# Layer 0 of a four-layer convolution network: the sums for dt over 32 columns of TensorE's array instead of 128

## The chip, the core and the metric

The kernel runs on one core of one Trainium2 chip. The time is device microseconds (us) of one execution, as the median of several; lower is better. Every time below comes from the timed runs or from one profiled execution; times inside that execution count from the start of its span.

## What is computed

The input x has 1024 channels of 64 x 64 pixels. Four layers follow each other, each of the form x = x + layer(groupnorm(x)). Only layer 0 is touched by the change. Cut to what matters, it is:

```
x_norm = layernorm2d(groupnorm(x))                       # per channel, over its 64 x 64 pixels
dt     = softplus(einsum('bsdc,c->bsd', x_norm, dt_w) + dt_b)   # one number for each channel s and image row d
log_a  = dt * (-exp(log_A))                              # one constant for each image row
out[t, r, c] = sum over j <= t of exp(cums[t, r] - cums[j, r]) * x_norm[j, r, c]   # cums = cumsum of log_a over channels
```

The channels are the sequence. out is a linear recurrence along them, h[t] = a[t, r] * h[t-1] + x_norm[t, r, :], with one decay a = exp(log_a) for each channel and image row, shared by the 64 pixels of the row. Layers 1 and 3 are 1024 x 1024 matrix products, layer 2 is a gated state-space layer with three such products; they take over at about 197 us and keep TensorE busy until the end.

## The kernel before, in words

**Tiles.** The image is split into two halves of 32 rows (TR = 32), and the channels into four groups of 256 (CH = 2 tiles of 128). One half of one channel group is a unit; there are NU = 8 units, and unit u is group u // 2, half u % 2. A unit's 2048 pixels form T0 = 16 pixel tiles of 128 pixels: 32 image rows times TW = 4 pixels of each. Four pixel tiles are a piece, so that there are NPIECE = 4 pieces to a unit and NI = 32 pieces in all. A piece is indexed i, with u = i // 4 and g = i % 4.

**Steps of a piece**, in the order in which they depend on each other:

- normalize (L590 on GpSimd, L592 on ScalarE) writes group-normed values xn for two pieces at a time, in two instructions of 128x1024.
- turn_in (L607, L613, L615): eight TensorE transposes of 128x128 turn xn so that pixels lie on partitions and channels along the free dimension. Four evictions of 128x256 apply the layer norm's weight and give XT, four pixel tiles of 256 channels. After the first pieces ScalarE does all four (L615).
- row_dt (L623): for each pixel tile one f32 product with a 128x128 matrix dtm as weights, accumulated over the 16 tiles of the unit into the left half of a PSUM bank called pd. dtm[t] holds dt_w on a block pattern (the constant "row": 1 where two pixels belong to the same image row), so that every one of a row's four partitions gets the row's sum. In the profile each such f32 product is two records, each with its weight load.
- decay, once a unit. Step 0: four ScalarE instructions on 128x256 (L632 to L635) make the two parts of softplus, e and m. Step 1: two TensorE products with the identity add them into the right half of the bank (L638). Step 2: ScalarE takes exp (L642, the first column alone, called first, and L643, the rest, into a PSUM tile called spread).
- begin, once a unit from the third on (L648, L651, GpSimd): multiplies the carried state by first and adds it to the first column of the unit's XT.
- scan (L658, VectorE): two 128x512 scans a piece, the recurrence itself, in place in XT.
- turn_back (L684; L676 and L682 in the last seven pieces): eight transposes back into PSUM (pb).
- add_up (L697, VectorE, two a piece; L695 on ScalarE for one of the two in the last pieces): adds the result to the image and sums it for the next layer's norm.
- squares (L709, ScalarE): one pass of 128x2048 for each channel tile of a finished unit, for the next layer's variance. Two a unit.

Beside this GpSimd sums weight blocks for layers 1 and 2 (L456 to L459, four instructions of 128x512 at a time), and VectorE takes the statistics (L567) for the norms of the later groups.

**Order.** The layer's scope sets the order by hand for TensorE, VectorE, ScalarE, GpSimd and the DMA queue of SyncE: each engine runs its instructions in the order in which the program issues them. The loop over i (from "for i in range(NI)") issues, for piece i: normalize for pieces i + 9 and i + 10 if i is odd; if g is 2, step 1 of the next unit's decay; scan(i); add_up(i - 1); turn_in(i + 7); row_dt(i + 6); turn_back(i); if g is 1, step 0 of the next unit's decay; if g is 2, step 2 of it and begin; one share of the weight sums; and, for g of 0 and 1 from the second unit on, squares of the unit before. The first seven pieces are turned in ahead of the loop, with their row_dt and the first unit's decay between them.

So pieces are turned in seven ahead of the scan, row_dt runs six ahead, and a unit's decay is ready two pieces before its first scan.

Of the kernel before, what the change touches and what calls it, by code (L numbers as in the profile page):

```python
# [10 lines left out]
F32 = mybir.dt.float32  # L11
# [9 lines left out]
P = 128  # L21
# [16 lines left out]
NK = -(-N // LT)  # L38
# [27 lines left out]
T0 = HN // P  # L66
TR = HW // 2
TW = HW // T0
CH = 2
NPIECE = T0 // 4  # L70
# [4 lines left out]
        ("Alog", S), ("D", 1), ("mob", 4 * HEADS), ("dbcb", HEADS * NF)]  # L75

_CST = [("ident", P), ("fold", LC), ("same", P), ("upto", LC), ("far", LC), ("eye", LC), ("eye8", S),
        ("from", 1), ("to", NK), ("group", P), ("row", P),
        ("gx", NT), ("gy", NT), ("flip", 7)]


def _columns(spec):
    at, out = 0, {}
    for name, n in spec:
        out[name] = slice(at, at + n)
        at += n
    return out, at
# [3 lines left out]
CST, NCST = _columns(_CST)  # L91
# [3 lines left out]
def tile_net(ctx: ExitStack, tc: tile.TileContext, x, par_d, cst_d, w_d, w2_d, dbcw_d, out):  # L95
    nc = tc.nc
# [414 lines left out]
    with tc.issue_after(exp_ln.ins), tc.tile_pool(name="l0x", bufs=2) as lx, \  # L511
# [4 lines left out]
        NU, NI = CT // CH * 2, CT // CH * 2 * NPIECE  # L516
# [27 lines left out]
        negA0 = const.tile([P, 2], F32, name="negA0")  # L544
        nc.scalar.activation(negA0, par[:, PAR["logA"]], AF.Exp)
        negA = const.tile([P, S], F32, name="negA")
        nc.scalar.activation(negA, par[:, PAR["Alog"]], AF.Exp)
        dtm = l0.tile([P, T0, P], F32, name="dtm", bufs=1)
        for t in range(T0):
            nc.gpsimd.tensor_scalar(dtm[:, t, :], cst[:, CST["row"]], pcol("dtw", t), None, ALU.mult)  # L550
        carry = l0.tile([P, 2, T0], F32, name="carry", bufs=1)
# [11 lines left out]
        def unit_stats(u, some):  # L563
            c, h = divmod(u, 2)
            for j in some:
                k, i = divmod(j, 4)
                nc.vector.bn_stats(stats[:, c * CH + k, 4 * h + i, :], half(u)[:, k, i * FB : (i + 1) * FB])  # L567
# [8 lines left out]
            nc.vector.tensor_copy(mean0[:, at], mean)  # L576
            nc.vector.tensor_scalar_mul(nmean0[:, at], mean, -1.0)

        xn, XT, PD, dt, PB = {}, {}, {}, {}, {}

        def normalize(n):

            u, j = divmod(n, 4)
            q, k = divmod(j, CH)
            scale, bias = norms[u // 2]
            xn[n] = l0.tile([P, 2, TR, HW // 4], F32, tag=f"xn{k}", name=f"xn{n}")
            part = half(u)[:, k, :].rearrange("p (r a g w) -> p a g r w", r=TR, a=2, g=2)[:, q]
            scale, bias = scale[:, k : k + 1], bias[:, k : k + 1]
            if n > LEAD + 4:
                nc.gpsimd.tensor_scalar(xn[n], part, scale, bias, ALU.mult, ALU.add)  # L590
            else:
                nc.scalar.activation(xn[n], part, AF.Identity, bias=bias, scale=scale)  # L592
# [24 lines left out]
        def row_dt(i):  # L617
            u, g = divmod(i, NPIECE)
            if g == 0:
                PD[u] = ps0.tile([P, FB], F32, tag="pd", name=f"pd{u}")  # L620
            for j in range(4):
                t = 4 * g + j
                nc.tensor.matmul(PD[u][:, : CH * P], dtm[:, t, :], XT[i][:, j, :], start=(t == 0), stop=(t == T0 - 1))  # L623

        def decay(u, step):

            if step == 0:
                e = l0.tile([P, CH * P], F32, tag="e", name=f"e{u}", bufs=1)
                m = l0.tile([P, CH * P], F32, tag="m", name=f"m{u}", bufs=1)
                dt[u] = e, m  # L630
                v = PD[u][:, : CH * P]
                nc.scalar.activation(e, v, AF.Abs, bias=pcol("dtb", 0))  # L632
                nc.scalar.activation(e, e, AF.Exp, scale=-1.0)
                nc.scalar.activation(m, v, AF.Relu, bias=pcol("dtb", 0))
                nc.scalar.activation(e, e, AF.Ln, bias=1.0)  # L635
            elif step == 1:
                for i, v in enumerate(dt[u]):
                    nc.tensor.matmul(PD[u][:, CH * P :], ident, v, start=(i == 0), stop=(i == 1))  # L638
            else:
                v, scale = PD[u][:, CH * P :], negA0[:, u % 2 : u % 2 + 1]  # L640
                if u > 1:
                    nc.scalar.activation(first_[u % 2], v[:, :1], AF.Exp, scale=scale)  # L642
                nc.scalar.activation(spread[u % 2][:, :, 1:], v[:, 1:].unsqueeze(1).to_broadcast([P, 2, CH * P - 1]),  # L643
                                     AF.Exp, scale=scale)
# [8 lines left out]
        def scan(i):  # L653
            u, g = divmod(i, NPIECE)
            c, h = divmod(u, 2)
            for j in (0, 2):
                xt = XT[i][:, j : j + 2, :].rearrange("p t c -> p (t c)")
                nc.vector.tensor_tensor_scan(xt, spread[h].rearrange("p t c -> p (t c)"), xt, 0.0, ALU.mult, ALU.add)  # L658
# [66 lines left out]
        turn_in(0, range(4))  # L725
        turn_in(1, range(4), "pb")
        row_dt(0)
        turn_in(2, (2, 3))
        row_dt(1)
        turn_in(3, (2, 3), "pb")  # L730
        row_dt(2)
        unit_stats(3, range(4))
        row_dt(3)
        decay(0, 0)
        normalize(4)
        unit_stats(3, range(4, 8))
# [16 lines left out]
        for i in range(NI):  # L753
            u, g = divmod(i, NPIECE)
            if i > 1 and i % 2 and i + LEAD + 2 < 4 * NU:
                normalize(i + LEAD + 2)
                normalize(i + LEAD + 3)
            if u + 1 < NU and g == 2:
                decay(u + 1, 1)
            scan(i)  # L760
            hand_on(i)
            if i == 0:
                finish_of(chain)
                chain = iter(())
            if i > 0:
                add_up(i - 1)
            if i == 0:
                for v, n in later.pop(0):
                    unit_stats(v, (n,))
                turn_in(5, (2, 3))  # L770
                turn_back(0)
                turn_in(6, (2, 3))
                row_dt(5)
            elif i + LEAD < NI:
                if i == 1:
                    row_dt(LEAD - 1)
                    turn_in(LEAD, (2, 3))
                    normalize(LEAD + 3)
                    normalize(LEAD + 4)
                turn_in(i + LEAD, ())  # L780
            if 0 < i <= NI - LEAD:
                row_dt(i + LEAD - 1)
            if i > 0:
                turn_back(i)
            if i == 0:
                normalize(LEAD + 1)
                normalize(LEAD + 2)
            if u + 1 < NU and g == 1:
                decay(u + 1, 0)
            if u + 1 < NU and g == 2:  # L790
                decay(u + 1, 2)
                if u > 0:
                    begin(u + 1)
            for v, n in later.get(i, ()):
                unit_stats(v, (n,))
            if i in (3, 11):
                chain = norm_chunk(2 if i == 3 else 3)
            next(chain, None)
            if i >= NPIECE and g < CH:
                squares(u - 1, g)  # L800
            if u == NU - 1 and 0 < g:
                for k in range(CH):
                    squares(u, k, g - 1)
            if g == 0 and u % 2 == 1:
                last_keep = keep(u // 2)
            if i == NPIECE + 1:
                bring(6)
            next(sums, None)
# [232 lines left out]
    with tc.manual_schedule(engines={E_.DVE, E_.PE, E_.Pool, E_.Activation}):  # L1041
        for i, _ in enumerate(pointwise("l1", W1, "b1", [3, 2] + EARLY, x0_d, x1_d, scores)):
# [35 lines left out]
    part, silus = {}, []  # L1078
# [21 lines left out]
    with tc.tile_pool(name="l2a", bufs=2) as pa, tc.tile_pool(name="l2a2", bufs=1) as pa2, \  # L1100
# [5 lines left out]
        row = pa2.tile([P, TPB, HEADS, NF2], F32, name="row", bufs=1)  # L1106
# [179 lines left out]
        with tc.manual_schedule(engines={E_.DVE, E_.PE, E_.Pool, E_.Activation}):  # L1286
# [3 lines left out]
            ends, i, chain, quiet = iter(()), -1, None, False  # L1290
# [71 lines left out]
    with tc.tile_pool(name="l2g", bufs=8) as pgat, tc.tile_pool(name="l2b", bufs=2) as pb, tc.tile_pool(name="l2r2", bufs=4) as prg, tc.tile_pool(name="l2h", bufs=1) as ph, \  # L1362
# [9 lines left out]
        rows, decay_, steps_ = {}, {}, {}  # L1372
# [463 lines left out]
def _constants():  # L1836
    c = np.zeros((P, NCST), np.float32)
    p, j = np.arange(P)[:, None], np.arange(P)[None, :]
    c[:, CST["ident"]] = p == j
    h, r = np.divmod(p, LC)  # L1840
    t = np.arange(LC)[None, :]
    c[:, CST["fold"]] = r == t
    c[:, CST["same"]] = h == j // LC
    c[:, CST["upto"]] = (t < S) | (r <= t)
    c[:, CST["far"]] = np.where((r >= S) & (t >= S) & (t < r), FAR, 0)
    c[:, CST["eye"]] = (r == t) & (r >= S)
    c[:KW, CST["eye8"]] = np.tile(np.eye(S), (KW // S, 1))
    c[:, CST["from"]] = HEADS * N + np.where(r < S, h * S + r, HEADS * S)
    c[:, CST["to"]] = HEADS * N + np.arange(NK)[None, :] * P + p
    c[:, CST["group"]] = (p // 32 == j // 32) / 32  # L1850
    c[:, CST["row"]] = p // TW == j // TW
    s = 1 - 2 * ((np.arange(P)[:, None] >> np.arange(6)[None, :]) & 1)
    s[:, 5] = 1
    c[:, CST["flip"]] = np.concatenate([s[:, :1], -s[:, :1], s[:, :5] * s[:, 1:]], axis=1)
    lin = _side()
    c[:, CST["gx"]] = np.tile(lin, HW).reshape(NT, P).T
    c[:, CST["gy"]] = np.repeat(lin, HW).reshape(NT, P).T
    return c
# [63 lines left out]
```

## Time and profile before

| what | value |
|---|---|
| median of 3 runs | 2637.35 us (2635.98 to 2638.56) |
| the profiled execution | 2640.7 us |
| its span | 2638.5 us, so 2.2 us lie around it |
| layer 0's last add_up ends | 189.8 us |
| first product of layer 1 starts | 197.0 us |
| busy share of the span: TensorE, VectorE, ScalarE, GpSimd | 97%, 69%, 40%, 46% |
| row_dt's products (L623) | 256 records, 64.1 us busy, all in the first 172 us |
| step 0 of decay (L632), starts for units 0 to 7 | 36.95, 58.61, 80.08, 97.75, 121.05, 138.72, 156.05, 171.28 us |

How to read the views used: the chain of waits goes back from the last instruction, at each step to what released it; its lines give start, length and what ran. The timeline lists an engine's instructions by start and length, with the idle time ahead of each and what ended it in square brackets. A table of windows gives the busy time of each engine in a stretch, with the number of records that began in it, the granted TensorE clock (PEclk, 1.00 is full) and the DMA share. A matmul's record lasts longer than its slot, since matmuls are pipelined: eight records of row_dt start one after the other over 1.73 us, while each is shown as about 0.4 us long. PE is TensorE, PEld its weight loads, DVE VectorE, ACT ScalarE, POOL GpSimd, SP SyncE.

### The profile page before, as it was taken

The page shows a single profiled execution, that of the slowest core. Times are in us where ns is not written, and L with a number is a line of the kernel's source. Part 1 is how long each engine was busy: PE and PEld are TensorE (multiplying, and loading weights), DVE is VectorE, ACT ScalarE, POOL GpSimd, SP SyncE. Part 2 cuts the span into 40 slices and gives each one's busy share as a digit, 9 for nine tenths or more (in the row PEclk, how much of TensorE's full clock was granted, in tenths as well). Part 3 has the DMA queues.
Part 4 walks back from the last instruction along what each step waited for, and adds up shares of the span by engine and source line. Part 5 has one row for each costly group of instructions (what it writes and reads, how often), then busy time and mean ns, then how long its engine had stood idle before and what let it go on. Part 6 is the DMA issues. An engine that isn't in the chain of part 4 may idle for free.

```text
span 2638.5 us, 30736 instructions
## 1 busy us (share of the span) xinstructions
PE 2560.3 (97%) x9588; PEld 1714.0 (65%) x9588; DVE 1819.1 (69%) x3776; ACT 1057.0 (40%) x1799; POOL 1217.9 (46%) x1102
## 2 busy tenths in 40 slices
PE   5889999999999999999999999999999999999999
PEld 5764444444555445544454558888888888788887
DVE  7986775664565554377877766576685775877877
ACT  4672010005655554476867662233233223312120
POOL 2453224322324242256464635576565665754544
PEclk9999999999999999999999999999999999999999
DMA  6555648655655676577677847899898798888896
GB/s 258 184 210 166 230 146 279 205 157 200 188 148 143 155 190 162 179 248 224 206 241 240 283 140 211 220 277 291 236 296 253 247 306 222 290 284 299 301 322 216
DMA packets 426996, 597.22 MB, mean 226 GB/s; under 512 B 142004, under 2 KB 210739, under 8 KB 423764
## 3 DMA queue, kind: packets, MB, share of 16 engines
q1 hardware_dynamic: 307268, 384.68, 46.0%
q10 hardware_dynamic: 91744, 136.85, 14.7%
q0 software_dynamic: 27824, 73.74, 11.7%
q8 instruction: 78, 1.28, 0.2%
q14 instruction: 82, 0.67, 0.1%
HBM read 435.10 MB, written 160.05 MB: 226 GB/s over the span
## 4 chain that ended last, share of the span: by engine, by line
PE 83%; DVE 8%; ACT 5%; POOL 1%; DMA 1%; issue 1%; SPq 0%; ACTq 0%; DVEq 0%; POOLq 0%
PE mm L892 38%; PE q_P2P L1793 6%; PE q_P3P L1793 5%; PE q_P1P L1793 5%; PE q_P5P L1793 5%; PE q_P6P L1793 5%; PE q_P4P L1793 5%; PE q_P7P L1793 5%; PE l2pt L1145 2%; PE py L1430 2%; DVE xt L658 1%; DVE cvp L1126 1%; ACT b L996 1%; DVE stats L567 1%; PE pd L623 1%
## 5 line engine op out<-in xcount | busy, mean ns | idle before, releaser
L892 PE MATMUL mm<-t,w 128*128 128x512 f32 x1536 | 681.0, 594 | 0.0
L892 PE MATMUL mm<-b,w 128*128 128x512 f32 x1152 | 513.6, 597 | 5.1 <-ACT b L996 4.0
L892 PEld LDWEIGHTS mm<-t,w 128*128 128x128 f32 x1536 | 285.8, 190 | 321.4 <-issue 313.6
L892 PEld LDWEIGHTS mm<-b,w 128*128 128x128 f32 x1152 | 215.6, 191 | 252.7 <-issue 240.7
L1439 POOL DMA_INDIRECT y_rows<-g,dst x74 | 74.1, 1001 | 181.8 <-ACT g L1435 169.9
L1126 DVE SCALAR_TENSOR_TENSOR cvp<-xs,par,cvp 128x512 f32<-128x512 f32 x128 | 95.4, 754 | 75.7 <-ACT cvp L1123 73.4
L1762 ACT COPY qQ<-q_P5P 128x512 f32<-128x512 f32 x48 | 28.1, 584 | 296.4 <-PE q_P5P L1793 269.0
L470 POOL TENSOR_TENSOR s<-s 128x256 f32<-128x256 f32 (+3 forms) x120 | 130.2, 1090 | 7.5
L1433 ACT COPY g<-py 8x512 f32<-8x512 f32 x146 | 83.8, 574 | 107.6 <-PE py L1430 106.6
L1177 DVE TENSOR_TENSOR xs<-mm,xs 128x512 f32<-128x512 f32 x64 | 41.8, 685 | 117.9 <-PE mm L892 117.9
L1153 POOL TENSOR_TENSOR acc<-l2xt,acc 128x136 f32<-128x136 f32 x56 | 29.3, 522 | 193.6 <-ACT l2xt L1147 192.7
L1013 DVE SCALAR_TENSOR_TENSOR image<-mm,par,image 128x512 f32<-128x512 f32 x64 | 47.0, 745 | 88.2 <-PE mm L892 88.2
L1145 PEld LDWEIGHTS l2pt<-both,cv 128*128 128x128 f32 x512 | 76.1, 190 | 34.6 <-issue 21.5
L850 POOL TENSOR_TENSOR t<-t,b 128x512 f32<-128x512 f32 x40 | 55.7, 1419 | 88.8 <-DVE t L850 85.4
L996 ACT ACTIVATE b<-image,gnl_bias,gnl_r_r 128x512 f32<-128x512 f32 x48 | 37.0, 808 | 145.4 <-PE mm L892 114.2
L1793 PE MATMUL q_P1P<-t_b,wq_P1P 128*128 128x256 f32 x384 | 92.0, 383 | 2.5 <-POOL t_b L1547 2.5
L1547 POOL TENSOR_TENSOR t_t<-qt 128x512 f32<-128x512 f32 x23 | 29.6, 1288 | 138.9 <-DVE qt L1547 72.4
L1793 PE MATMUL q_P5P<-t_t,wq_P5P 128*128 128x256 f32 x384 | 92.2, 383 | 0.4 <-POOL t_t L1547 0.4
L1793 PE MATMUL q_P4P<-t_t,wq_P4P 128*128 128x256 f32 x384 | 90.9, 380 | 1.4 <-DVE qV L1770 1.4
L1551 ACT ACTIVATE qb<-x_x_b,gn_bias,gn_r_r 128x512 f32<-128x512 f32 x64 | 48.8, 808 | 107.3 <-DVE qQ L1722 36.0
L1770 DVE TENSOR_TENSOR qV<-q_P4P,qV 128x512 f32<-128x512 f32 x96 | 64.8, 686 | 37.7 <-PE q_P4P L1793 36.0
L1793 PE MATMUL q_P6P<-t_t,wq_P6P 128*128 128x256 f32 x384 | 90.7, 379 | 0.0
(432 smaller groups left out, 5962.6 us busy)
## 6 DMA issues: line engine op xcount, KB each, us to landing
w<-s_d SPq DMA_DIRECT2D x96, 512.0 KB, 4.3
w<-in_w_dram SPq DMA_DIRECT2D x72, 512.0 KB, 4.7
x_x_b<-x_d ACTq DMA_DIRECT2D x28, 1024.0 KB, 6.4
image<-x_d SPq DMA_DIRECT2D x12, 2048.0 KB, 12.4
wq_P6P<-s_d SPq DMA_DIRECT2D x84, 256.0 KB, 4.3
wq_P7P<-s_d SPq DMA_DIRECT2D x84, 256.0 KB, 5.5
wq_P5P<-s_d SPq DMA_DIRECT2D x84, 256.0 KB, 3.1
wq_P3P<-s_d SPq DMA_DIRECT2D x84, 256.0 KB, 3.6
```

Of the source, the lines that this page charges most:

```text
L470: eng.tensor_tensor(out, a, b, ALU.subtract)
L850: eng.tensor_tensor(B[name][k], B[one][k], B[two][k], ALU.subtract)
L892: nc.tensor.matmul(to[o], w[:, k, o * P : (o + 1) * P], B[name][k], start=(fresh and k == 0), stop=(k == KH - 1), skip_group_check=True)
L996: nc.scalar.activation(t, X[nb][:, ct, :], AF.Identity, bias=bias, scale=scale)
L1126: nc.vector.scalar_tensor_tensor(cv, xo[:, at + t : at + t + FB], pcol("dww", 3 * o + t), cv, ALU.mult, ALU.add)
L1145: nc.tensor.matmul(pt[:, q * NV : (q + 1) * NV], cv[:, (q0 + q) * P : (q0 + q + 1) * P], both[:, o, :], start=True, stop=True)
L1430: nc.tensor.matmul(py, G2[k % 2], rows[k][:, :DH], start=True, stop=True)
L1433: nc.scalar.copy(rows[k + 1][h * LC : h * LC + S, :DH], py[h * LC : h * LC + S])
L1439: nc.gpsimd.indirect_dma_start(out=y_views[k % len(y_views)][:, :], out_offset=bass.IndirectOffsetOnAxis(ap=dst_[:, k : k + 1], axis=0), i ...
L1551: nc.scalar.activation(tile_of(j, name)[:, k], held[j, "x", name][:, k], AF.Identity, bias=bias, scale=scale)
L1770: nc.vector.tensor_tensor(to, ps, to, ALU.add)
L1793: nc.tensor.matmul(ps[:, o, :], w[:, k, o * P : (o + 1) * P], rhs[:, k, :], start=(new and o == 0 and k == 0), stop=(k == 1), skip_group_c ...
```

## The change

Four things change, all in layer 0.

1. **row_dt.** dtm becomes 128x32 for each pixel tile: one column for an image row. The four pixel tiles of a piece go to four groups of 32 columns of the array, and so to partitions 0 to 31, 32 to 63, 64 to 95 and 96 to 127 of the bank. Each group accumulates over the four pieces of the unit. There are as many products as before, each with a quarter of the columns.
2. **Two new steps a unit.** own_rows copies the four partial sums (128x256) from PSUM to SBUF on ScalarE. all_rows is one f32 product with the new constant "rows" (1 where partition p modulo 32 is the image row of output j); it adds the four groups and gives each row's sum to its four partitions, in the right half of the bank. decay then reads the right half and adds its two parts into the left half, where it did it the other way round.
3. **Order.** For g of 1, own_rows is issued ahead of turn_back and all_rows behind it. The squares of that piece, which stood behind step 0 of decay, now stand ahead of it, so that ScalarE's order is: evictions of turn_in, own_rows, squares, step 0. Step 1 of decay keeps its place, ahead of the next piece's turn_in. For the first two units there are no such squares.
4. **Sizes.** GpSimd's 16 instructions that build dtm write 128x32 in place of 128x128. The constants grow from 922 to 954 columns.

On TensorE and ScalarE this is eight instructions more each (one a unit); the order on VectorE, GpSimd and SyncE is the same, and nothing changes behind layer 0.

```
-        ("from", 1), ("to", NK), ("group", P), ("row", P),
+        ("from", 1), ("to", NK), ("group", P), ("row", TR), ("rows", P),
...
-        dtm = l0.tile([P, T0, P], F32, name="dtm", bufs=1)
+        dtm = l0.tile([P, T0, TR], F32, name="dtm", bufs=1)
...
-                nc.tensor.matmul(PD[u][:, : CH * P], dtm[:, t, :], XT[i][:, j, :], start=(t == 0), stop=(t == T0 - 1))
+                nc.tensor.matmul(PD[u][j * TR : (j + 1) * TR, : CH * P], dtm[:, t, :], XT[i][:, j, :],
+                                 start=(g == 0), stop=(g == NPIECE - 1))
+
+        def own_rows(u):
+            part[u] = l0.tile([P, CH * P], F32, tag="m", name=f"part{u}", bufs=1)
+            nc.scalar.copy(part[u], PD[u][:, : CH * P])
+
+        def all_rows(u):
+            nc.tensor.matmul(PD[u][:, CH * P :], cst[:, CST["rows"]], part[u], start=True, stop=True)
...
-                v = PD[u][:, : CH * P]
+                v = PD[u][:, CH * P :]
...
-                    nc.tensor.matmul(PD[u][:, CH * P :], ident, v, start=(i == 0), stop=(i == 1))
+                    nc.tensor.matmul(PD[u][:, : CH * P], ident, v, start=(i == 0), stop=(i == 1))
...
         row_dt(3)
+        own_rows(0)
+        all_rows(0)
         decay(0, 0)
...
             if 0 < i <= NI - LEAD:
                 row_dt(i + LEAD - 1)
+            if u + 1 < NU and g == 1:
+                own_rows(u + 1)
             if i > 0:
                 turn_back(i)
...
             if u + 1 < NU and g == 1:
+                all_rows(u + 1)
+                if i >= NPIECE:
+                    squares(u - 1, g)
                 decay(u + 1, 0)
...
-            if i >= NPIECE and g < CH:
+            if i >= NPIECE and g < CH and not (g == 1 and u + 1 < NU):
                 squares(u - 1, g)
...
-    c[:, CST["row"]] = p // TW == j // TW
+    c[:, CST["row"]] = p // TW == j[:, :TR]
+    c[:, CST["rows"]] = p % TR == j // TW
```

More of the change, by code (lines that the diff above doesn't have):

```diff
@@ L577, in norm_chunk @@
             nc.vector.tensor_scalar_mul(nmean0[:, at], mean, -1.0)
-        xn, XT, PD, dt, PB = {}, {}, {}, {}, {}
+        xn, XT, PD, dt, PB, part = {}, {}, {}, {}, {}, {}
         def normalize(n):
@@ L637, in decay @@
                 for i, v in enumerate(dt[u]):
-                    nc.tensor.matmul(PD[u][:, CH * P :], ident, v, start=(i == 0), stop=(i == 1))
+                    nc.tensor.matmul(PD[u][:, : CH * P], ident, v, start=(i == 0), stop=(i == 1))
             else:
-                v, scale = PD[u][:, CH * P :], negA0[:, u % 2 : u % 2 + 1]
+                v, scale = PD[u][:, : CH * P], negA0[:, u % 2 : u % 2 + 1]
                 if u > 1:
```

## The prediction

> **What bounds the kernel now.** I read the chain of waits first, for the first 420 us. Behind 197 us it is TensorE alone, in products that the change does not touch; layer 0 fills the time ahead of that, so what counts is when its last add_up ends (189.8 us). VectorE is the busiest engine there. The table of windows shows where it has idle time left:
>
> ```profile
> 80.00:95.00 15.00, 13.23 (x86) 11.54 (x85) 14.89 (x31) 12.04 (x23) 8.75 (x14) 1.00 0.76 284
> 95.00:108.00 13.00, 11.91 (x75) 10.47 (x75) 13.00 (x24) 10.19 (x22) 7.04 (x13) 1.00 0.23 77
> ...
> 122.00:140.00 18.00, 15.92 (x100) 14.14 (x100) 15.35 (x33) 14.46 (x30) 11.24 (x17) 1.00 0.38 129
> 140.00:158.00 18.00, 16.04 (x101) 14.44 (x102) 14.91 (x27) 14.50 (x29) 11.23 (x17) 1.00 0.48 175
> ```
>
> The columns are PE, PEld, DVE, ACT and POOL. From 80 to 108 us VectorE works all the time (27.9 of 28); from 122 to 158 us it idles 5.7 of 36, and so does every other engine. A loop over several engines sets the pace there, and the chain shows it:
>
> ```profile
> 138.72 0.48 ACT e L632
> ...
> 140.31 1.71 ACT junk_None L709
> 142.11 0.19 ACT junk_None L709
> 142.30 1.82 ACT xt L615 x4
> 144.44 0.32 POOL carry L648
> ...
> 149.49 1.27 POOL s_a L459
> 150.77 2.37 POOL xn L590 x2
> 153.18 1.11 PE xpt L607 x7
> 154.29 1.74 PE pd L623 x8
> 156.05 0.48 ACT e L632
> ```
>
> One turn of the loop is a unit: step 0 of decay, squares, evictions, first, then on GpSimd begin, the weight sums and normalize, then the transposes of the normalized pieces, and the next step 0. The starts of carry (L648) are 17.34 us apart from unit 2 to 3 (86.12, 103.46), 17.35 from 4 to 5 (127.09, 144.44) and 17.33 from 5 to 6 (161.77). GpSimd truly waits in it:
>
> ```profile
> 144.44 0.32 POOL L648 TENSOR_SCALAR carry<-carry,first 128x16 f32<-128x16 f32 x1 [5.78 <-ACT first L642]
> ```
>
> **The products of row_dt.** Eight records a piece take 1.73 us, 0.216 each. Below, all four column groups overlap and two slots remain, 0.43 us. Above, none overlaps, 1.73 us. A change of the array's shape must be added; the nearest row is one of layer 1, two transposes of another shape between dense products:
>
> ```profile
> 385.61 0.27 PE sort L370 x2
> ```
>
> Two records and the way back cost 0.27 us, so a piece costs 0.70 to 2.0 us. Between them lies 1.35: the two records of a product use the same 32 columns, so they follow each other, and if records also start in the order of the program, five slots of eight are left (1.08, and 0.27). No row tells 0.70 from 1.35; I take 1.0, and keep both ends.
>
> The Trainium skill, page "TensorE: Matmul & The Clock Gate", section "Part 3: Packing small matmuls — row/col tiling", gives 2.38 times for three column tiles, which would make 1.73 into 0.73. The page "TensorEngine Tiling (Array Packing)", section "Key Properties", says against it that a change of tiling mode drains the array. No run yet shows a column group.
>
> **Is this on the path?** In the loop, hardly: ScalarE's evictions of turn_in end at 138.50 us and pd at 138.70, so own_rows, which is behind these evictions on ScalarE, can start 0.2 us earlier at most, however short the products are. They count at two places. In the opening, TensorE runs pd from 27.41 to 36.93 us nearly without a gap. With 1.0 a piece, the last eviction by VectorE falls from 34.5 to about 32.8, pd ends at about 34.0; own_rows (0.48, as an eviction of 128x256) and all_rows (0.43, and 0.28 until it is readable) come on top, so step 0 starts at about 35.2 in place of 36.95, and the first scan 1.6 us earlier: **-1.6** (-2.2 with 0.70, +1.5 with 2.0). Around 112 us the clock is at half and pd takes 3.41 us on the chain; 1.0 becomes 1.8 there: **-1.6** (-2.2 to 0).
>
> **The new steps and the new order.** From the end of the evictions (call it E) to carry it takes 5.94 us now (138.50 to 144.44): step 0 (1.55), squares (2.08), evictions (1.93), which are ready when squares end, since step 1 and the transposes ran beside squares. That cover is moved: squares now stand beside all_rows, and behind step 0 ScalarE has nothing until TensorE has done step 1 and half a turn_in. Unit 1, which has no squares between, shows that wait in the kernel before:
>
> ```profile
> 61.91 1.93 ACT L615 ACTIVATE xt<-xpt,par 128x256 f32<-128x256 f32 x4 [1.69 <-PE xpt L607]
> ```
>
> So after the change: own_rows 0.48, squares 2.08, step 0 1.55, the wait 1.69, evictions 1.93, first until carry 0.30; 8.03 in place of 5.94, **2.1 us more a turn**. Behind the waiting step 1 on TensorE stand turn_in, row_dt and turn_back, for which ScalarE and VectorE wait in turn. all_rows itself (done about 1.1 us after E) is hidden by squares; without them it would be 0.7 more, as in units 0 and 1, where VectorE's statistics (2.4 us a piece) cover it.
>
> Then the **clock**. Between all_rows and step 1 TensorE has nothing for about 3 us (from 1.1 to 4.1 after E); now its gap there is 0.81 us. A table of 1.7 us windows of TensorE shows what such gaps did:
>
> ```profile
> 67.60:69.30 1.70, 0.92 (x9) 1.00 0.05 18
> 69.30:71.00 1.70, 0.92 (x6) 1.00 0.00 0
> ...
> 107.00:108.70 1.70, 0.72 (x6) 1.00 0.41 154
> 108.70:110.40 1.70, 0.92 (x6) 1.00 0.66 245
> 110.40:112.10 1.70, 0.56 (x3) 0.56 0.59 218
> 112.10:113.80 1.70, 1.70 (x7) 0.50 0.18 77
> ```
>
> With 1.84 us busy in 3.4 the clock stayed, with 1.64 it went to half at 110.6 and came back at 117.4; another fall lasted from 42.3 to 45.7. The new gap leaves 0.6 to 1.5 busy in most stretches of 3.4 us, so I expect half clock when step 1 and the transposes run. pd at half clock (3.41 for 1.73) prices that: step 1 from 0.87 to 1.7, the first four transposes 0.4 later (1.16 from start to eviction at 111.54, 0.74 at 162.22), 1.2 us together; I take 1.0, as not every unit will be caught.
>
> The page named first, section "Part 1: The HAM clock gate", has a free-running window of 3.413 us and a fall after an idle one; the 3.4 and 6.8 us here agree. By "idle" taken at its word a gap of 3 us fills no window and the clock stays, which would make my sum 4.2 us less; the row at 107.00 fell with 1.64 us of work, and I go by the row.
>
> **The sum**, against the profiled execution (2640.7 us). Opening -1.6. Unit 2's chain is 2.1 to 3.1 longer, but VectorE is behind there anyway: nothing. Unit 3's comes on top, so that its first is 3.7 to 5.8 later against VectorE's work; the eight transposes of turn_back that VectorE needs at 105.72 come 1.0 later without the clock's fall and up to 4 with it: +2.2. Around 112 us -1.6. Unit 4: step 0 was 0.67 late there already for pd, so +1.5, and 1.0 for the clock: +2.5. Units 5 and 6: 2 x (2.1 + 1.0) = +6.2. After that normalize is done and the loop is gone. VectorE is dense from 161.98 on, except for 1 to 1.5 us; it resumes 0.4 to 1 us sooner after first because pd is shorter, and the last unit's later step 0 about eats the rest: -1.2. Together -1.6 + 2.2 - 1.6 + 2.5 + 6.2 - 1.2 = **+6.5**, 2647.2 for an execution like the profiled one. That one lies 3.35 us above the median, so **2644** (2637.35 + 6.5). GpSimd's dtm (16 x 0.594, done by 19.2 us, needed at 27) and the 32 columns of constants cost nothing: work ahead of 21.5 us waits for data and norms.
>
> **Rivals.** *The clock stays up.* The mechanism is the threshold in the stretch between all_rows and step 1: if it is under the 0.6 to 1.5 us of work that are left, 1.0 falls away in units 4, 5 and 6 and 1.2 at unit 3, so +2.3, 2640, not slower by what can be told. It decides once less than 3 of these 4.2 us are paid. For it: 1.84 of 3.4 kept the clock, so the edge is sharp and unknown below. *The column groups don't overlap*, the change not doing what it says: 2.0 a piece, so opening +3.1, 112 us +1.6, and pd ends 0.5 behind the evictions in three units, +1.5; +12.7, 2650. For it: no row shows an overlap. *Faster:* the loop is not what binds, GpSimd's 5.8 us wait is slack, and 2.1 a turn is hidden. Then the two gains and the end stay, -4.4, and a little of VectorE's idle time, to -6: 2631. Against it: three equal turns, and TensorE waiting 0.98 us for xn in the middle of a turn.
>
> **Chances.** Forecast 0.50, clock stays 0.25, no overlap 0.13, faster 0.12. Runs of this kernel differ so that 0.2% (5.3 us) is about what can be told from no change. The forecast's own spread is +3 to +10, so 0.36 of it counts as slower; with 0.13 and 0.03 that is 0.52. Same: 0.14, 0.22 and 0.04 of the last, 0.40. Faster: 0.08. The range, 2636 to 2651, takes in the first three cases and leaves out the last and the far ends.
>
> **What will show it.** Starts of carry 19.4 us apart or more for units 4 to 6 (20.5 with the clock), ScalarE idle 1.7 us or more between step 0 and the evictions in each unit, half clock at step 1, pd at 0.7 to 1.35 us a piece, step 0 of unit 0 at about 35 us. Turns of 17.3 us would prove me wrong on the order, and pd at 2 us on the array.

## The result and the profile after

| | before | after |
|---|---|---|
| median of 4 runs | 2637.95 us (2635.98 to 2638.56) | 2651.07 us (2644.65 to 2653.26) |
| ratio | | 1.0044, 95% interval 1.0032 to 1.0056 |
| the profiled execution, its span | 2640.7, 2638.5 | 2644.65, 2642.9 |
| carry starts, units 2 to 7 | 86.12, 103.46, 127.09, 144.44, 161.77, 175.76 | 87.58, 108.37, 129.60, 149.77, 169.68, 182.92 |
| layer 0's last add_up has ended (start of the sum behind it on VectorE) | 189.85 | 197.39 |
| first product of layer 1 starts | 196.98 | 205.44 |

The kernel became slower by 0.44%, 11.6 us of 2638 (the two medians are 13.1 us apart). The forecast had the sign and +6.5. The execution that was profiled is the fastest of the four of after, so its span (+4.4) tells less than the median. In it layer 0's last add_up ends 7.5 us later and the first product of layer 1 starts 8.5 us later, and the rest took 4.1 us less than in the profiled execution of before (2437.4 against 2441.5, from that product to the end of the span), though nothing there was changed. More of that below.

First the table of windows of after, in the same stretches (columns: stretch, length, busy PE, PEld, DVE, ACT, POOL, the granted clock, DMA share, GB/s):

```profile
80.00:95.00 15.00, 10.52 (x76) 7.84 (x76) 14.11 (x29) 11.13 (x24) 7.29 (x11) 0.89 0.62 236
95.00:108.00 13.00, 9.81 (x53) 7.00 (x54) 10.42 (x19) 7.54 (x16) 4.21 (x8) 0.74 0.31 95
...
122.00:140.00 18.00, 12.97 (x93) 9.93 (x91) 14.88 (x31) 12.90 (x26) 10.27 (x16) 0.88 0.41 141
140.00:158.00 18.00, 13.25 (x96) 9.41 (x95) 12.55 (x23) 13.50 (x26) 9.04 (x14) 0.88 0.28 102
```

The clock column, 1.00 in all four rows of before, is 0.74 to 0.89. In the stretch left out, 108 to 122 us, it is the other way round: 0.76 before and 0.93 after. VectorE, which was busy throughout from 80 to 108 us, now idles 3.5 of these 28 us: the loop sets the pace there too. From 122 to 158 us every engine has more idle time than before.

The chain of waits of after, over one turn of the loop:

```profile
129.60 0.32 POOL carry L656
...
135.91 2.37 POOL xn L590 x2
...
138.32 1.76 PE xpt L607 x7
140.09 1.01 PE pd L623 x8
141.10 1.90 PE pb L692 x8
143.00 0.87 PE pd L631 x2
...
143.89 0.48 ACT e L640
...
145.54 1.13 PE pd L646 x4
146.67 0.85 PE xpt L607 x7
...
149.77 0.32 POOL carry L656
```

It is the loop of before, 20.17 us long in place of 17.35. From carry to the end of normalize nothing is longer. Then two things are. Between transposes and step 0 the chain now goes on through TensorE for two steps more, and the clock is at half there, so that the pieces take 1.6 to 2.2 times their usual length: transposes 1.76 (1.11 before), row_dt 1.01 (0.57 at full clock), eight transposes of turn_back 1.90 (0.87 in before, where they were not on this stretch of the chain), and all_rows 0.87 on top. And behind step 0 comes a second passage through TensorE (step 1 and transposes, 1.13 and 0.85 us) ahead of the evictions, where squares had filled ScalarE's time.

### The profile page after: what moved, and what is told of

It reads as the page before. It is cut to its first block, busy times and chain, and to the rows that moved or that the text cites. A ratio compares the mean times of both kernels' runs of the same rounds, so it can differ in the third digit from the quotient of the medians.

```text
span 2642.9 us, 30781 instructions
## 1 busy us (share of the span) xinstructions
PE 2542.9 (96%) x9604; PEld 1681.0 (64%) x9604; DVE 1813.4 (69%) x3776; ACT 1060.4 (40%) x1807; POOL 1214.0 (46%) x1102
## 3 DMA queue, kind: packets, MB, share of 16 engines
q0 software_dynamic: 27824, 73.74, 11.6%
## 4 chain that ended last, share of the span: by engine, by line
PE 83%; DVE 7%; ACT 6%; POOL 1%; issue 1%; DMA 1%; SPq 0%; DVEq 0%; ACTq 0%; POOLq 0%
PE mm L907 38%; PE q_P2P L1808 6%; PE q_P3P L1808 5%; PE q_P5P L1808 5%; PE q_P1P L1808 5%; PE q_P7P L1808 5%; PE q_P4P L1808 5%; PE q_P6P L1808 5%; PE py L1445 2%; PE l2pt L1160 2%; DVE cvp L1141 1%; ACT b L1011 1%; DVE xt L666 1%; DVE stats L567 1%; PE xpt L607 1%
## 5 line engine op out<-in xcount | busy, mean ns | idle before, releaser
L1808 PE MATMUL q_P7P<-t_t,wq_P7P 128*128 128x256 f32 x384 | 90.7, 379 | 0.0
```

Source lines behind the costliest of these rows:

```text
L1808: nc.tensor.matmul(ps[:, o, :], w[:, k, o * P : (o + 1) * P], rhs[:, k, :], start=(new and o == 0 and k == 0), stop=(k == 1), skip_group_c ...
```

## What the experiments were for

The theory as it stood after the result: the order costs some 2 us a turn (squares moved away from where they covered step 1 and the transposes), half clock some 1 us more, and the column groups themselves are a gain. Rivals: the groups themselves cost time (no overlap, or a price for changing the array's shape); the two new steps cost it; the clock is a bystander. Each ratio is to runs of before on the same chip; the chips differ between some rows. In the table, "turns" are the distances of carry from unit 4 to 5 and from 5 to 6, in the profiled execution.

| kernel | ratio to before, 95% interval | turns | layer 0 ends | clock, 122 to 172 us |
|---|---|---|---|---|
| before | 1 | 17.35, 17.33 | 189.85 | 1.00 |
| after | 1.0044 [1.0032, 1.0056] | 20.17, 19.91 | 197.39 | 0.85 |
| after again | 1.0039 [1.0025, 1.0053] | 20.20, 21.25 | 200.15 | 0.77 |
| order alone | 1.0025 [1.0016, 1.0034] | 19.00, 20.19 | 196.95 | 0.93 |
| groups alone | 0.9985 [0.9976, 0.9994] | 17.00, 17.01 | 183.81 | 0.93 |
| new steps and order, no groups | 1.0066 [1.0052, 1.0080] | 21.09, 19.54 | 207.30 | 0.93 |
| new steps and groups, old order | 1.0030 [1.0019, 1.0040] | 19.73, 20.05 | 194.65 | 0.86 |
| after with filler | 1.0033 [1.0021, 1.0045] | 19.44, 19.16 | 195.08 | 1.00 |
| before, weight sums a piece earlier | 0.9996 [0.9987, 1.0005] | 15.87, 16.20 | 186.98 | 1.00 |
| after, weight sums a piece earlier | 1.0008 [0.9999, 1.0018] | 18.65, 17.51 | 193.50 | 0.86 |
| the same, squares on both sides | 1.0001 [0.9992, 1.0010] | 16.74, 16.03 | 192.42 | 0.90 |
| the same, with filler | 0.9993 [0.9984, 1.0002] | 16.76, 15.20 | 189.42 | 1.00 |
| old order, weight sums a piece earlier | 0.9994 [0.9985, 1.0003] | 15.15, 15.50 | 186.62 | 0.97 |
| the same, with filler | 0.9981 [0.9972, 0.9990] | 15.16, 15.24 | 185.81 | 1.00 |

The shift of layer 0's end in one profile and the shift of the time by the ratio agree within about 4 us in every row, most closely in the two largest (no groups: +17.5 and +17.4; after again: +10.3 and +10.3).

## The parts, one at a time

**After again.** The same kernel, unchanged.

> The changed kernel once more, for the spread of its runs, which was 2644.7 to 2653.3 us. Theory (order and clock): about +0.4% to +0.5%, with runs several us apart, since half clock falls in windows that do not start with the kernel; its profile shows turns of 19.4 to 21 us for units 4 to 6. Rival (the time is lost behind layer 0): a run much slower than the profiled one has the same end of layer 0 (197.3 us) and loses the rest later.

Median 2648.42 us (2647.61 to 2650.68) against 2638.84. The result repeats. In this execution the last add_up ends at 200.15, 10.3 us later than before. So one kernel's layer 0 spreads by almost 3 us from one execution to the next (197.39 and 200.15), and the clock differs with it, 0.85 and 0.77. The rival is out for this pair: the spans differ by 5.3 us, and 3.8 of these have been lost by the first product of layer 1 (205.44 and 209.19).

**The order alone**, in the kernel before:

```
             if u + 1 < NU and g == 1:
+                if i >= NPIECE:
+                    squares(u - 1, g)
                 decay(u + 1, 0)
...
-            if i >= NPIECE and g < CH:
+            if i >= NPIECE and g < CH and not (g == 1 and u + 1 < NU):
                 squares(u - 1, g)
```

> The kernel before with one edit: the squares of g = 1 stand ahead of step 0. No column groups, no new steps. Theory (the order costs): evictions to carry 0.2 + 2.08 + 1.55 + 1.69 + 1.93 + 0.3 = 7.75 us in place of 5.94, so turns of about 19.1 us and +5 to +8 us in all. Rival (column groups or the two new steps cost it): turns stay at 17.3 us and the time within 1 us of before.

Ratio 1.0025, turns of 19.00 and 20.19 us, at a clock of 0.93: the order alone makes more than half of the loss (0.25% of 0.39 to 0.44%), without any new step or column group. The timeline of ScalarE in this kernel shows, behind step 0 of unit 5 (142.50 to 144.11), the wait that the prediction took from unit 1:

```profile
145.87 0.56 ACT L615 ACTIVATE xt<-xpt,par 128x256 f32<-128x256 f32 x1 [1.75 <-PE xpt L607]
```

1.75 us for the 1.69 that was forecast.

**The groups alone.** The products go to four column groups; there is no own_rows, no all_rows, and the order is that of before. This kernel leaves out the sum over the four groups, so its output is not the layer's; it serves for the time alone.

```
-                nc.tensor.matmul(PD[u][:, : CH * P], dtm[:, t, :], XT[i][:, j, :], start=(t == 0), stop=(t == T0 - 1))
+                nc.tensor.matmul(PD[u][j * TR : (j + 1) * TR, : CH * P], dtm[:, t, :], XT[i][:, j, :],
+                                 start=(g == 0), stop=(g == NPIECE - 1))
```

> The column groups alone: neither own_rows nor all_rows, squares where they were; decay reads the four groups' own partial sums, so the sum over the groups and its spreading are left out. Theory: the products themselves are a gain, step 0 of unit 0 about 3 us earlier and pd short at half clock, turns of 17.1 to 18.3 us (half clock in TensorE's longer waits): -4 to 0 us. Rival (column groups or their clock are what costs): +5 us or more.

Ratio 0.9985: the groups are a gain of 0.15%, 4.0 us, and the interval lies wholly below 1. Turns are 0.3 us shorter, and step 0 of unit 0 starts at 33.46 in place of 36.95. The rival that the groups themselves cost time is out.

**No groups, the rest of the change.** After, with products of 128 columns again, so that all_rows copies through the identity.

```
-                nc.tensor.matmul(PD[u][j * TR : (j + 1) * TR, : CH * P], dtm[:, t, :], XT[i][:, j, :],
-                                 start=(g == 0), stop=(g == NPIECE - 1))
+                nc.tensor.matmul(PD[u][:, : CH * P], dtm[:, t, :], XT[i][:, j, :], start=(t == 0), stop=(t == T0 - 1))
...
-            nc.tensor.matmul(PD[u][:, CH * P :], cst[:, CST["rows"]], part[u], start=True, stop=True)
+            nc.tensor.matmul(PD[u][:, CH * P :], ident, part[u], start=True, stop=True)
```

> The changed kernel with its new order and both new steps, but the products of row_dt with 128 columns as before (all_rows multiplies by the identity). Theory: turns of 19.6 us (2.1 for the order, 0.2 for pd's end), no gain in the opening (step 0 of unit 0 at about 38 us), half clock rarer since TensorE is denser: +7 to +11 us. Rival (the column groups are what costs): within 2 us of before.

Ratio 1.0066, 17.4 us, more than expected. Against the order alone that is 0.41% more, for the two new steps, and the groups take 0.2 to 0.3% of it back. Where the new steps cost it shows early: step 0 of units 0, 1 and 2 starts at 38.40, 61.52 and 85.94, against 37.41, 59.07 and 81.65 with the order alone.

**New steps and groups, old order.** In after, the squares go back behind step 0.

```
                 all_rows(u + 1)
-                if i >= NPIECE:
-                    squares(u - 1, g)
                 decay(u + 1, 0)
...
-            if i >= NPIECE and g < CH and not (g == 1 and u + 1 < NU):
+            if i >= NPIECE and g < CH:
                 squares(u - 1, g)
```

> The changed kernel with the squares of g = 1 back behind step 0, so that they cover step 1 and the transposes and nothing covers all_rows. Theory: evictions to carry 0.37 + 1.0 + 1.55 + 2.08 + 1.93 + 0.3 = 7.2 us, turns of 18.6 us without the clock, 19.5 with it; +1 to +6 us. Rival (the order is harmless): same as the changed kernel or slower by 1 us a turn, since all_rows is now bare.

Half of the expectation failed. The turns are 19.73 and 20.05, hardly shorter than those of after. The timeline shows why:

```profile
137.83 1.97 PE L692 MATMUL pb<-cst,xt 128*128 128x128 f32 x8
...
140.36 0.47 ACT L640 ACTIVATE e<-pd,par 128x256 f32<-128x256 f32 x1 [2.03 <-PE pd L631]
```

ScalarE has done own_rows at 138.33, but eight transposes of turn_back, at half clock, stand ahead of all_rows, and ScalarE waits 2.03 us for it. The two squares passes of a unit are at g of 0 and 1, and only that at g of 1 stands here: it can cover the passage through TensorE ahead of step 0 or the one behind it, not both, and each costs about 2 us bare. So at this place the order is a choice between two nearly equal losses, and the change costs a turn 2 us or more whichever is taken. It follows that the order alone, taken as a cause, was half the story: without new steps it is a plain loss, with them it is a trade.

By ratios, the groups are -0.15%, the new steps +0.41 to +0.45% (no groups less order alone; this kernel less groups alone), the order +0.25% without the new steps and +0.09 to +0.14% with them (after less this kernel). The intervals of these last two overlap, but their runs on one chip differ by 3.0 us in the mean, give or take 1.9, so that the old order is a little better.

## The clock

Windows of 1.7 us of TensorE alone, in after (stretch, length, busy with the number of records, granted clock, DMA share, GB/s):

```profile
133.30:135.00 1.70, 1.19 (x12) 1.00 0.41 154
135.00:136.70 1.70, 0.00 (x0) 1.00 0.76 282
136.70:138.40 1.70, 0.56 (x2) 0.65 0.76 246
...
143.50:145.20 1.70, 0.36 (x1) 0.85 0.00 1
```

The clock does fall in each unit, and in units 4 to 6 not where the prediction put it. TensorE, done sooner with row_dt, runs dry in the middle of the turn: it waits for normalize, and the timeline of TensorE has the rows

```profile
137.15 0.49 PE L607 MATMUL xpt<-cst,xn 128*128 128x128 f32 x1 [2.66 <-POOL xn L590]
138.32 1.76 PE L607 MATMUL xpt<-cst,xn 128*128 128x128 f32 x7 [0.69 <-POOL xn L590]
```

where before, in the same unit, had

```profile
134.67 0.39 PE L607 MATMUL xpt<-cst,xn 128*128 128x128 f32 x1 [0.15 <-POOL xn L590]
135.85 1.11 PE L607 MATMUL xpt<-cst,xn 128*128 128x128 f32 x7 [0.79 <-POOL xn L590]
```

From 133.8 to 137.2 us, the 3.4 us ahead of the fall, it worked for 0.75 us. Unit 6 is alike (2.67 us of waiting for normalize); ahead of unit 4's fall, at 120.1 us, TensorE waits 1.90 us for VectorE's group statistics instead. In the windows left out TensorE is busy throughout at 0.50: in unit 5 half clock covers the transposes, row_dt, turn_back and all_rows, and is over when step 1 runs at 145.54 (1.13 us on the chain). Only in units 2 and 3 was step 1 caught (1.95 and 2.07 us on the chain).

**After with filler** settles whether the clock is a cause or a bystander: products whose result nobody reads keep TensorE busy in these two gaps, from unit 2 on, two of 128x512 behind all_rows and three ahead of the transposes of a piece with g = 1.

```
+        def fill(i, n):
+            pt = psum.tile([P, FB], F32, tag="tp", name=f"fill{i}_{n}")
+            for _ in range(n):
+                nc.tensor.matmul(pt, ident, cst[:, :FB], start=True, stop=True)
...
+                if g == 1 and i >= 2 * NPIECE:
+                    fill(i, 3)
                 turn_in(i + LEAD, ())
...
                 all_rows(u + 1)
                 if i >= NPIECE:
+                    fill(i, 2)
                     squares(u - 1, g)
```

> The changed kernel with products that nobody reads in TensorE's two waits of a turn: two of 128x512 behind all_rows from unit 2 on, and three ahead of the transposes of g = 1 from i = 9 on. They keep TensorE busy and wait for nothing that isn't there. Theory (half clock costs about 1 us a turn): full clock from 96 us on, turns of 19.4 us in place of 20, 3 to 5 us faster than the changed kernel and runs closer together. Rival (the clock does not matter, only the order): the same time or up to 2 us slower.

The clock was 1.00 from 122 to 172 us, and the turns 19.44 and 19.16 us, against 20.17 and 19.91 (and 20.20 and 21.25 in the second profile of after). So half clock costs 0.7 us a turn by the mean of the first, 1.4 by the second, where 1.0 was forecast. The chain of this kernel, over the part that half clock had stretched (transposes, squares, step 0):

```profile
137.50 0.64 PE xpt L607 x3
...
140.43 1.99 ACT junk_None L722 x2
142.42 0.37 ACT e L645
```

Now the squares (L722 here) cover all_rows fully, as the prediction had it, and the turn is the one worked out there: 17.34 + 2.1 = 19.4. So what is left at full clock, 1.8 to 2.1 us a turn, is the order's, with own_rows in it. Over the whole execution the 3 to 5 us that were expected of the filler did not come: 1.0033 against 1.0039 and 1.0044, with overlapping intervals, can't be told from no gain.

## The loop

The prediction said that the loop through GpSimd sets the pace. Then work taken off GpSimd between carry and normalize must shorten the turn. The four weight-sum instructions there (5.3 us) belong to a fixed sequence; one share issued ahead of the loop moves every later share to the piece before:

```
+        next(sums, None)
         for i in range(NI):
```

**In the kernel before:**

> The kernel before with its weight sums one piece earlier (g = 1 in place of g = 2), so that GpSimd does them while it waits for first and not between begin and normalize. Theory (a loop through GpSimd sets the turn): 5.3 us leave the loop, the turn falls from 17.3 us to what TensorE needs, 15.3 to 15.8; -3 to -6 us. Rival (VectorE or ScalarE sets the turn): turns stay near 17 us and the time within 1 us.

The turns fall from 17.35 and 17.33 to 15.87 and 16.20, and the chain from 128 to 160 us has no GpSimd in it any more: it runs through TensorE for somewhat more than half of a turn (138.62 to 147.37 us) and through ScalarE for the rest. A piece of it:

```profile
139.75 0.95 PE xpt L607 x8
140.71 1.73 PE pd L623 x8
142.44 0.87 PE pb L684 x8
```

TensorE is busy for 15.06 us of the first of these turns (15.87), so it is close to being the bound, and row_dt at 1.73 us is on the path for two of a unit's four pieces: the place where column groups would pay. The total, for which 3 to 6 us were expected, moved by 1.3 us only (ratio 0.9996, no change within its interval), though this profile's layer 0 ends 2.9 us sooner.

**In after:**

> The changed kernel with the weight sums one piece earlier. Theory: 5.3 us leave the loop, which would be 14.5 us; ScalarE's own work of a turn (14.8 us, 0.4 for own_rows, and 1.7 of waiting between step 0 and the evictions) sets it at 16.5 to 17 us: 8 to 12 us faster than the changed kernel, -3 to +2 us against before. Rival (VectorE sets the turn): the same as the changed kernel.

1.0008 in place of 1.0039 to 1.0044; turns of 18.65 and 17.51, longer than the 16.5 to 17 expected. Most of the loss is gone, but the change is still not a gain. With the loop through GpSimd loosened, ScalarE's bare wait behind step 0 remains, and it is 3.35 and 3.08 us long in these turns, since here half clock does catch step 1 (2.07 us on the chain both times), which is where the prediction had put it.

**Squares on both sides**, in after with the weight sums earlier: the pass of g = 0 moves to behind step 0, that of g = 1 stays ahead of it.

```
                     squares(u - 1, g)
                 decay(u + 1, 0)
+                if i >= NPIECE:
+                    squares(u - 1, 0)
...
-            if i >= NPIECE and g < CH and not (g == 1 and u + 1 < NU):
+            if i >= NPIECE and g < CH and u + 1 == NU:
                 squares(u - 1, g)
```

> The changed kernel with the weight sums one piece earlier and with the other squares of a unit (those of g = 0) moved behind step 0, so that one pass of squares covers all_rows and the other step 1. Theory: no bare wait is left on ScalarE; its own work sets the turn, 14.8 + 0.4 us and little more, so 15.4 to 16.5 us; with the opening 2 us earlier this beats the kernel before by 4 to 8 us (0.15% to 0.3%), and the kernel with the sums alone moved by 1 to 5 us. Rival (the extra ScalarE and TensorE steps cost what they cost wherever they stand): no better than the changed kernel with its sums moved, about +0.1%.

Both waits are covered but for 0.73 us in unit 6, and the turns are 16.74 and 16.03, but the total is level with before (1.0001) and not faster, so the expectation missed. Units 2 and 3 start late (carry at 89.28 and 108.16), and the end of layer 0 is only 1.1 us sooner than without this edit.

**The same with filler** (three of 128x512 behind all_rows):

> The kernel of the run before with three products of 128x512 that nobody reads behind all_rows from unit 2 on, to hold TensorE's clock up. Theory: 2.6 us of work in a wait of about 3.5 us, so half clock disappears there, 1 to 3 us faster than without them. Rival (with the covers in place the clock is off the path): the same within 1 us, or slower where the wait is shorter than the filling.

0.9993 [0.9984, 1.0002]; clock 1.00 from 122 to 172 us, layer 0 ends 3.0 us sooner than without filler, and the runs, on the same chip, are 3.3 us shorter in the mean, give or take 2.0: the expectation held. Against before it is no change within its interval.

**Old order, weight sums earlier**, which is the kernel "new steps and groups, old order" with the one line of the weight sums:

> The changed kernel with the squares of g = 1 back behind step 0 and the weight sums one piece earlier. Theory: evictions to carry as in the kernel with the squares back alone (about 7.5 us), the 5.3 us of sums off the loop, so ScalarE sets the turn at 15.5 to 16 us, and units 1 to 3 start earlier than with the squares ahead; end of layer 0 at 184 to 188 us, -3 to -6 us against before and 1 to 3 us ahead of the kernel before with its sums moved. Rival (own_rows and all_rows eat what the column groups give): level with the kernel before with its sums moved, or slower.

Turns of 15.15 and 15.50, the shortest so far, and 0.9994: from 1.0030, one line took 0.36%. With TensorE no longer waiting for normalize, the clock holds at 0.97, turn_back ahead of all_rows takes its full-clock time in these two turns, and the old order's bare wait shrinks from 2.03 to 0.79 us. But the total missed the 3 to 6 us expected: it is level with before, weight sums a piece earlier (0.9996; layer 0 ends at 186.62 and 186.98), which is what the rival said.

**The same with one filler product** behind all_rows, from unit 2 on:

> The kernel of the run before with one product of 128x512 that nobody reads behind all_rows from unit 2 on (0.87 us in a wait of about 1.7). Theory: half clock gets rarer, up to 2 us faster. Rival (the clock is off the path once the sums are): the same within 1 us.

2633.04 us against 2639.13, ratio 0.9981 [0.9972, 0.9990]: faster than before by 5.0 us of 2637, and so than after, which was slower. One piece on TensorE's timeline, first in "before, weight sums a piece earlier":

```profile
140.54 1.89 PE L623 MATMUL pd<-xt,dtm 128*128 128x256 f32 x8
...
144.11 1.89 PE L623 MATMUL pd<-xt,dtm 128*128 128x256 f32 x8
```

and then in this kernel:

```profile
140.04 0.64 PE L623 MATMUL pd<-xt,dtm 128*32 128x256 f32 x8
140.61 1.09 PE L697 MATMUL pb<-cst,xt 128*128 128x128 f32 x8
...
142.60 0.64 PE L623 MATMUL pd<-xt,dtm 128*32 128x256 f32 x8
```

The starts are what counts: from row_dt to the next row_dt it is 3.57 us there and 2.56 here. A unit has four pieces, but the turns are only 0.7 to 1.0 us shorter. TensorE no longer sets the pace: it is busy for 13.20 us of a turn of 15.16, VectorE for 13.73 and ScalarE for 13.92. And own_rows (0.27 us of the chain) and all_rows stand bare at the end of a turn:

```profile
150.90 0.71 PE pd L631 x2
```

This is the form in which the column groups pay, by a little: against before with the weight sums alone earlier it is 0.15% (0.9981 for 0.9996, on two chips; 0.02 to 0.28% by an estimate from the two intervals), with the filler in it. What each of its three edits is worth was tried only in this order. The filler's part is shown, as the runs of the two kernels, on one chip, differ by 4.1 us in the mean, give or take 2.2; but layer 0 ends only 0.8 us sooner with it in the profiles (185.81 for 186.62), so where the rest is gained stays open.

## Why the prediction came out as it did

- **What binds** (the loop through GpSimd): right. Taking 5.3 us of GpSimd's work out of it shortened the turns of both kernels by 1.1 to 2.4 us. Of the three equal turns that were named for it, though, the first (86.12 to 103.46) is no witness: the chain of before runs through VectorE alone there.
- **Products of a piece, 1.0 us taken, 0.70 to 2.0 as bounds**: the lower bound was the answer. A piece of the loop is 1.0 us shorter (3.57 to 2.56), so 1.73 became 0.73: 0.57 from its first record to the next instruction's, 0.10 longer ahead of it (transposes to row_dt 1.06 for 0.96) and 0.06 behind it (turn_back to transposes 0.93 for 0.87). All four groups overlap, and with 0.43 for two slots the change of shape, to and fro, costs 0.30 where 0.27 was counted. The rival "no overlap" is out. The value between, 1.0, was chosen for want of a row; it made no difference to the sign, since the products are not on the loop's path. The measured median lies nearer to the 2650 of "no overlap" than to the forecast, and only these rows tell the two apart.
- **Opening, -1.6**: -1.5 measured (first scan 41.65 to 40.16), partly by luck. Step 0 of unit 0 started at 34.64, not 35.2, as the shorter products gave more; with 0.73 a piece the forecast would have been about -2.2. But the first scan does not wait for step 0. In both kernels it follows the group statistics on VectorE without a gap, and these start behind VectorE's last eviction, which ended 1.8 us sooner. With the groups alone step 0 came 1.2 us sooner still (33.46), and the first scan no sooner (40.24).
- **Unit 2 nothing, unit 3 +2.2**: the step that failed most in size: +3.8. The group statistics on VectorE (L183) that open this stretch are 1.55 us sooner than before (67.51 for 69.06), those that close it 2.23 later (110.95 for 108.72). The forecast rested on VectorE being behind anyway. The windows of after show that cover used up: VectorE idles 3.5 us there.
- **Around 112 us and unit 4, -1.6 and +2.5, +0.9 together**: +0.3 (from the +2.23 just named to +2.51 for carry of unit 4).
- **Units 5 and 6, +6.2**: +5.4 (carry of unit 6 7.91 late, from 2.51), turns of 20.17 and 19.91 against 20.5.
- **The end, -1.2**: -0.4, to 7.54 at the last add_up. These are +7.5 in this profile for +6.5 in the sum, and +10.3 in the second one.
- **The clock**: that it falls was right, and the price of about 1 us a turn; the mechanism was the half of it that was wrong. The prediction looked at the new gap between all_rows and step 1, and that gap brought half clock to step 1 in units 2 and 3 only. In units 5 and 6 the fall comes from the gap ahead of it, where TensorE, faster now, waits 2.66 us for normalize, and in unit 4 from the wait for group statistics. The edge that was read from two stretches of before (1.84 us of work kept the clock, 1.64 lost it) does not hold either. The 3.41 us that end with before's falls, at 110.60 and 42.33 us, have 1.45 and 2.36 us of work in them, and with the order alone 1.50 us in 3.41 (142.26 to 145.67) kept full clock. What decides is open. The rival "clock stays" is out.
- **all_rows hidden by squares**: nearly. It takes 0.71 us bare at full clock, as forecast (0.43 + 0.28), and own_rows 0.37 where 0.48 was counted. At half clock turn_back and all_rows outlast squares by 0.36 us (step 0 at 143.89). With the clock held, squares cover it.
- **The total**: 2644 forecast for 2651.07, at the upper edge of the range (2651). In layer 0 the sum was 1 to 4 us short. The rest is not explained by a step. Of the profiled pair, the part behind layer 0 ran 4.1 us less than before's; in the profile of the second runs of after it took 2439.0, and over all fourteen profiles 2437.4 to 2445.3. Part of this shows in the records: behind layer 0, before has three falls of the clock of 3.41 us each (near 1575, 2295 and 2312 us), after one (2301), and each costs up to 1.7 us. Over the fourteen profiles the part behind layer 0 grows with their number: 2437.4 to 2439.0 us with none or one (six profiles), 2439.4 to 2442.7 with two (five), 2441.5 and 2444.4 with three, 2445.3 with four. That these falls make the run-to-run spread of the kernels stays an argument, as nothing was run that changes them alone.

## What to carry to other kernels

Where a loop over several engines sets the pace, price an edit by what each engine's queue has to do while it waits: here one pass of squares could cover only one of two passages through TensorE, so that a change made for shorter products cost 0.4%. Before shortening an engine's work, ask what ends its idle time next; if the answer is another engine, the saved time becomes a wait, and on TensorE perhaps also half clock. First loosen the loop (one line moved the weight sums), then shorten the work that it uncovers.

## What the runs showed of the hardware

- Four column groups of 128x32 f32 products with 256 moving columns, two records each, all accumulating in one PSUM bank, start their eight records in 0.57 us instead of 1.73, and cost 0.73 with the change of the array's shape on both sides. The Trainium skill, page "TensorE: Matmul & The Clock Gate", section "Part 3: Packing small matmuls — row/col tiling", gives 2.38 times for three column tiles. Measured here, for four tiles and with the change of shape in it, are 1.73 / 0.73 = 2.4 times.
- Less work on TensorE lowered its own clock, and so did a longer wait. With the groups alone the clock from 122 to 172 us went from 1.00 to 0.93, and with the order alone, the products being as before, to 0.93 too; in after, 0.85, five products a unit that nobody reads brought it back to 1.00. Lengths at half clock in layer 0 are multiples of 3.41 us (3.41 to 20.48 in these profiles), and within a profile the falls lie whole multiples of 3.41 us apart (42.33 and 110.60 us in before). A stretch of that length need not be empty for a fall: 0.75 us of work in after (133.8 to 137.2 us) and 2.36 in before (38.9 to 42.3) were followed by one, 1.50 with the order alone was not, so the busy time that the profile shows does not tell which.
